# First attention chunk of each image: six additions into the totals moved behind the first slot, two inner sums ahead of it, the last filling's steps split

## The chip, the core and the metric

The kernel runs on one core of a Trainium2 chip. The metric is the device time of one execution in microseconds. Five engines work side by side, each through its own instructions in order: PE (TensorE, matrix products), DVE (VectorE), ACT (ScalarE), POOL (GpSimd) and SP (SyncE). DMA transfers are issued from the queues of SP, ACT and POOL.

## What is computed

Two layers over x of shape (2, 512, 64, 64) in float32. Layer 0 is a deformable convolution on the group-normalized x, added to x. Layer 1, which this change touches, is an attention over the 4096 pixels of each image:

```python
q = jnp.tanh(px @ Wq.T)
k = jnp.tanh(px @ Wk.T)
v = px @ Wv.T
scores = jnp.einsum('bip,bjp,p->bij', q, k, align_w)
attn = jax.nn.softmax(scores, axis=2)
content = px + attn @ v
content = content @ Wfc.T + bfc
```

It is followed by a batch normalization over both images, a ReLU and the addition of the layer's input.

## The kernel before

Layer 0 fills the first 1160 us of the span. Layer 1 then takes the two images one after the other (loop over `n`). For each image there are two stages.

**The value stage.** Four steps `i`, each over two chunks of 512 pixels, compute keys and queries (`pk`), and in four tiles `t` the values already multiplied by `Wfc` (`values`, products `pvx` and `pvy`, L1740). The values are kept in a form for a fast matrix product with seven products in place of eight at two levels: VectorE combines the pieces of two tiles in a generator `filling`, eight steps per pair of tiles, and stores them in DRAM by SP's queue (L1386, L1387). `fill` is a queue of such generators, and `step(count)` runs that many of their steps. `between(1)` and `between(2)` are called by `values` in the midst and at the end of a tile, and each ends in `step(2)`. The steps of the last pair (group 7) are left over when the stage ends.

**The slots.** A `Chunk` is 1024 of the queries, and there are four chunks for each image. Each has 63 slots: seven forms of the fast product (`p`), by eight groups of keys and the residual (`g`). Slot `s` does seven products on PE into `accx` and `accy` (`products`, L1544). It needs a piece `v` from DRAM (`fetch`, three slots ahead, on ACT's queue for the first six slots of an image and on SP's after), a piece of exponentials `e`, and the inner sums `tt` of that piece (`inner_sums`, L1523 and L1524 on VectorE). `sums(s)` makes the inner sums of slot `s`. It runs `LEAD` = 4 slots ahead, and the tiles rotate through five buffers, which they share with the stored sums `vsum` of `filling`.

The exponentials come from `produce`: PE makes scores `pS` (L1451), ACT their exponentials (L1456). They come two pieces at a time at the slots in `EVENTS`, by rows e0, e2, e3, e1. For the first chunk of an image, e0 and e2 are produced in the value stage (`EARLY`). At the next event or slot, `settle` lets VectorE subtract one half of a piece from the other (`transform`, L1441), and for e0 and e2 adds the piece into a running total of the softmax's denominators (`add_total`). That addition is a DMA that accumulates, or, where `direct` is set, one on VectorE:

```python
if direct:
    nc.vector.tensor_add(parts[0], parts[0], t)
else:
    nc.gpsimd.dma_start(parts[0], t, accum_op=ALU.add)
```

`direct` is set for what is produced in the value stage's last step (`i == 3`). In slot 4 the two running totals are merged (`merge`, L1490) and folded (`total`, L1494, L1495). In slot 5, `spread_total` lets PE sum them over the partitions into `pr` (L1499), ahead of that slot's products. The residual of the chunk is loaded on POOL's queue (`at(-7, ...)`), normalized on ACT (`at(-3, ...)`, four instructions L1335) and scaled by `pr` on VectorE (L1515). The second row's total goes the same way in slots 20 to 23.

All of layer 1 stands under a manual schedule: the order of the instructions on each engine is the order in which the program calls them.

Of the kernel before, what the change touches and what calls it, by code (L numbers as in the profile page):

```python
# [529 lines left out]
LEAD = 4  # L530
# [24 lines left out]
def window_path(  # L555
# [70 lines left out]
    with ExitStack() as l0:  # L626
# [384 lines left out]
        class Chain:  # L1011


            def __init__(self, stage, i):
                self.steps = stage(i) if 0 <= i < NSEQ else iter(())
# [219 lines left out]
    with ExitStack() as l1, tc.manual_schedule():  # L1235
# [78 lines left out]
        with ExitStack() as inner:  # L1314
# [106 lines left out]
            class Chunk:  # L1421

                def __init__(self, n, k):
                    self.n, self.k = n, k
                    self.end = n + 1 == NB and k + 1 == NCH // 2
                    self.order = END if self.end else ORDER
                    self.e, self.tot, self.m, self.q = {}, {}, {}, None

            ROW = {"e0": (0, 0), "e1": (0, 1), "e2": (1, 0), "e3": (1, 1)}
            ORDER = (("e0", 0), ("e2", 1), ("e1", 6), ("e3", 4), ("e3", 2), ("e0", 3), ("e2", 5))  # L1430
# [47 lines left out]
            def settle(c, key, g, direct=False):  # L1478

                for k in (g, g + 1):  # L1480
                    e = c.e[key, k]
                    transform(e)
                    if key in ("e0", "e2"):
                        add_total(c, 0, e, direct)
                    if key == "e1":
                        second_row(c, k)

            def merge(c, qh):
                t, u = c.tot[qh]
                nc.vector.tensor_add(t, t, u)  # L1490
# [141 lines left out]
            class Attention:  # L1632
# [45 lines left out]
                def slot(self, s):  # L1678
                    k, l = divmod(s, SLOTS)
                    c = self.chunks[k]  # L1680
                    nxt = self.chunks[k + 1] if k + 1 < NCH // 2 else None
                    self.fetch(s + 3)
                    if l % (NG + 1) == 0 and self.ends:
                        next(self.ends[-1], None)
                    if l == 20:
                        merge(c, 1)
                    self.before(l, c)
                    if nxt and l >= 43:
                        if l == 43:
                            nxt.q = load_queries(self.n, k + 1)  # L1690
                        self.before(l - SLOTS, nxt)
                        self.at(l - SLOTS, nxt, s)
                    self.at(l, c, s)
                    if l == 21:
                        total(c, 1)
                        self.sums(s + 3)
                    if l + LEAD not in (8, 24, 26):
                        self.sums(s + LEAD)
                    if l == 4:
                        merge(c, 0)  # L1700
                        total(c, 0)
                    p, g = divmod(l, NG + 1)
                    products(c, p, g, self.v.pop(s), self.t.pop(s))
                    for e in self.ends[:-1] if g == 0 else self.ends:
                        next(e, None)
                    if g == NG:
                        self.ends = self.ends[-1:] + [collect(c, p, first_copy(c), c.acc)]
# [102 lines left out]
            for n in range(NB):  # L1810
                at = Attention(n)
                first = at.chunks[0]

                for i in range(NCH // 2):
                    if 0 < i < 3 or n and i == 0:
                        k = i + 1 if i else 1
                        pixels[k] = load_pixels(n, k, nc.gpsimd)
                    pk = pair_bank("pk")
                    for h in range(2):
                        for kb in range(KB):  # L1820
                            nc.tensor.matmul(  # L1821
                                pk[:, h, :], wkq[:, kb, h : h + 2].rearrange("p h d -> p (h d)"),
                                pixels[i][h][kb // 2][:, kb % 2, :], start=(kb == 0), stop=(kb == KB - 1),
                            )
                    qt = piece("qt", (P, CH))
                    for h in range(2):
                        rk, rq = slice(h * DQ, (h + 1) * DQ), slice((1 - h) * DQ, (2 - h) * DQ)
                        nc.scalar.activation(qt[rq], pk[rq, h, :], AF.Tanh)
                        nc.scalar.activation(keys[rk, i, :], pk[rk, h, :], AF.Tanh)
                    nc.scalar.activation(qt, qt, AF.Identity, scale=al)  # L1830
                    for h in range(2):
                        nc.scalar.dma_start(q_d[n][i][:, h, :], qt[(1 - h) * DQ : (2 - h) * DQ, :])
                    if i == 0:
                        first.q = load_queries(n, 0)
                    if i:
                        psums[i] = sum_pixels(nc.vector, pixels[i])
                    for t in range(4):
                        if t % 2 == 0:
                            raw = []
                        raw.append(piece("vform", (P, 2, 4, P)))  # L1840

                        def between(stage):
                            event = EARLY.get((i, t))
                            if event and stage == 2:
                                for done in at.open:
                                    settle(*done)
                                produce(first, *event)
                                at.open = [(first, *event, i == 3)]
                            step(2)

                        values(t, pixels[i], psums[i], wc, wcs, raw[-1], between)
                        if t in (1, 2) and i + 1 < NCH // 2:
                            for h in range(2):
                                normalize(pixels[i + 1][t - 1][h], 2 * h, *norms[n])
                        if t % 2:
                            g = 2 * i + t // 2
                            fill.append(filling(*raw, v_d[n][g], piece if g + 1 == NG else None))
                        if i == 3 and t == 2:
                            for s in range(3):
                                at.fetch(s)  # L1860
                    pixels.pop(i)
                    psums.pop(i)
                for s in range(LEAD):
                    at.sums(s)
                for s in range(NCH // 2 * SLOTS):
                    if s == 0:
                        at.at(-7, first, s)
                    if s == 2:
                        at.at(-3, first, s)
                    at.slot(s)  # L1870
                    if s < 5:
                        step(2)
                    if n == 0 and s in (92, 94, 96, 98, 101, 103):
                        next(later, None)
                    l = s - (NCH // 2 - 1) * SLOTS
                    if n + 1 < NB:
                        if l == 47:
                            pixels[0] = load_pixels(n + 1, 0, nc.gpsimd)
                        if l == 49:
                            wc = value_output(nc.sync)  # L1880
                        if l == 51:
                            wcs = sum_value_output(wc)
                        if l in (52, 53):
                            for h in range(2):
                                normalize(pixels[0][l - 52][h], 2 * h, *norms[n + 1])
                        if l == 55:
                            psums[0] = sum_pixels(nc.vector, pixels[0])
                    if n + 1 == NB:
                        check(l)
                    if n + 1 == NB and l >= 22:  # L1890
                        if l == 48:
                            for _ in batch_norm(0):
                                pass
                        if l > 49:
                            put_out(True)
                        if l in (54, 57, 60):
                            put_out(True)
                        if l > 51:
                            refill(nc.gpsimd)
                        if l == 22:  # L1900
                            room = key_tile()
                            spare = deque((room[:, 0:2], room[:, 2:4]))
                        live = 3 + sum(last + g >= l for last in (31, 36, 45, 54) for g in range(NG + 1))
                        if waiting and (spare or live + len(taken) + 2 <= 37):
                            fetch(lambda name: spare.popleft() if spare else ring_piece(name), nc.gpsimd)
# [67 lines left out]
```

## Time and profile before

| | |
|---|---|
| median of 3 runs | 3325.03 us (3322.0 to 3329.67) |
| the profiled execution's own time | 3324.42 us |
| its span | 3322.5 us |
| mean granted clock of PE | 0.98 |
| PE busy | 3144.2 us (95% of the span) |
| DVE busy | 2747.2 us (83%) |
| ACT busy | 1342.1 us (40%) |
| POOL busy | 292.2 us (9%) |
| value stage of image 0, first slot after it | 1162 to 1304 us, 1304.24 us |
| value stage of image 1, first slot after it | about 2208 to 2349 us, 2349.28 us |

A row of the time view gives the start in us from the span's start, the duration, the engine, the line of the kernel, the operation, what it writes and reads, the shapes, and in brackets the idle time of the engine ahead of it with what ended it. A row of the waits gives the waiting engine and instruction, what it waited for, the sum in us, the number of waits and the longest. A row of the windows gives the stretch, its length, the busy time and number of instructions of PE, PE's weight loads, DVE, ACT and POOL, the granted clock of PE, the share of the DMA engines in use, and GB/s.

### The profile page before, as it was taken

What the parts mean: (1) busy time and instruction counts of PE and PEld (TensorE: products, weight loads), DVE (VectorE), ACT (ScalarE), POOL (GpSimd) and SP (SyncE); (2) the same over time, 40 slices, a digit from 0 to 9 for tenths busy, and PEclk for the clock granted to TensorE, in tenths of its full rate; (3) what the DMA queues carried; (4) which work ended last, traced back from release to release, by engine and by line L of the source; (5) the groups of instructions that cost most, each with busy time, mean ns of one, the idle gap of its engine ahead of it and who ended that gap; (6) DMA issues with size and microseconds to landing.
All of it is one profiled execution on the core that took longest, in us unless ns stands there. A gap on an engine that the chain in (4) does not pass through costs nothing. (4 is left out here: it accounts for less than half of the span.)

```text
span 3322.5 us, 38350 instructions
## 1 busy us (share of the span) xinstructions
PE 3144.2 (95%) x14171; PEld 2259.2 (68%) x14171; DVE 2747.2 (83%) x3928; ACT 1342.1 (40%) x1848; POOL 292.2 (9%) x420
## 2 busy tenths in 40 slices
PE   5899999999999899999999999999999999999991
PEld 2455555555555676787877877887687787787781
DVE  7999999999998689885976967968897786886994
ACT  2678887888886533203113122123211202203114
POOL 1100000000000000001000011000001101001022
PEclk9999999999999999999999999999999999999996
DMA  7335543443444278658667677557667758658699
GB/s 240 121 118 155 153 122 112 137 151 108 120 137 139 92 287 258 196 171 224 196 175 215 190 219 202 187 191 245 220 201 207 203 179 239 189 161 238 195 349 374
DMA packets 241237, 632.61 MB, mean 190 GB/s; under 512 B 28528, under 2 KB 45552, under 8 KB 240016
## 3 DMA queue, kind: packets, MB, share of 16 engines
q1 hardware_dynamic: 177136, 415.33, 37.7%
q0 software_dynamic: 51936, 179.86, 20.4%
q10 hardware_dynamic: 11968, 34.87, 2.8%
q8 instruction: 114, 1.87, 0.2%
q14 instruction: 83, 0.68, 0.1%
HBM read 410.15 MB, written 124.91 MB: 161 GB/s over the span
## 5 line engine op out<-in xcount | busy, mean ns | idle before, releaser
L1544 PE MATMUL accy<-tt,v 128*128 128x256 f32 x2016 | 601.7, 380 | 0.7 <-DVE ct L1577 0.6
L1456 ACT ACTIVATE e<-pS 128x1024 f32<-128x1024 f32 x256 | 248.3, 1021 | 737.2 <-PE pS L1451 737.2
L1544 PE MATMUL accx<-e,v 128*128 128x256 f32 x1792 | 471.2, 385 | 0.3 <-ACT e L1456 0.3
L1544 PE MATMUL accy<-e,v 128*128 128x256 f32 x1792 | 461.7, 380 | 0.0
L1544 PEld LDWEIGHTS accy<-tt,v 128*128 128x128 f32 x2016 | 383.8, 191 | 54.2 <-DVE ct L1577 1.0
L1544 PEld LDWEIGHTS accx<-e,v 128*128 128x128 f32 x1792 | 333.5, 190 | 120.4 <-issue 77.7
L806 DVE SCALAR_TENSOR_TENSOR conv<-xn,L_conv_dw_w_sb,conv 128x504 f32<-128x504 f32 (+1 forms) x512 | 376.8, 744 | 29.7 <-ACT conv L798 15.8
L1544 PEld LDWEIGHTS accy<-e,v 128*128 128x128 f32 x1792 | 341.7, 191 | 46.8
L1524 DVE TENSOR_TENSOR tt<-tt,e 128x512 f32<-128x512 f32 x448 | 309.9, 692 | 15.3
L1544 PE MATMUL accx<-tt,v 128*128 128x256 f32 x1008 | 301.2, 380 | 13.1 <-DVE tt L1523 13.1
L1523 DVE TENSOR_TENSOR tt<-e 128x256 f32<-128x256 f32 x448 | 187.7, 419 | 144.8 <-PE accy L1544 142.3
L976 PEld LDWEIGHTS pa<-bt,patch 96*128 96x128 f32 x2048 | 247.6, 195 | 58.1 <-issue 38.2
L976 PE MATMUL pa<-bt,patch 96*128 96x128 f32 x2048 | 251.8, 279 | 8.4 <-issue 3.6
L1451 PE MATMUL pS<-q,keys 64*128 64x512 f32 x1024 | 254.7, 615 | 0.3 <-DVE stats L1729 0.3
L962 ACT COPY bt<-pb 96x1024 f32<-96x1024 f32 x120 | 225.9, 2023 | 50.4 <-PE pb L957 50.4
L772 PE MATMUL pq<-in_w,xn 128*128 128x512 f32 x512 | 234.0, 599 | 3.6 <-ACT xn L762 3.5
L996 PE MATMUL py<-dT,L_conv_out_w_sb 128*128 128x512 f32 x512 | 230.0, 593 | 0.0
L1544 PEld LDWEIGHTS accx<-tt,v 128*128 128x128 f32 x1008 | 191.9, 191 | 40.3 <-DVE tt L1523 14.3
L1549 ACT COPY u<-accx 128x256 f32<-128x256 f32 x56 | 20.8, 372 | 484.2 <-PE accx L1544 477.6
L866 PE MATMUL po<-om_w_pg,feat 128*128 128x432 f32 x512 | 206.4, 548 | 0.8 <-ACT feat L849 0.8
L987 ACT COPY dT<-pa 32x256 f32<-32x256 f32 x496 | 179.9, 363 | 62.9 <-PE pa L976 53.6
L996 PEld LDWEIGHTS py<-dT,L_conv_out_w_sb 128*128 128x128 f32 x512 | 95.5, 190 | 114.3 <-issue 107.4
(274 smaller groups left out, 4266.4 us busy)
## 6 DMA issues: line engine op xcount, KB each, us to landing
v<-wv SPq DMA_DIRECT2D x436, 448.0 KB
tot<-e POOLq DMA_DIRECT2D x160, 512.0 KB, 6.8
patch<-xt SPq DMA_DIRECT2D x256, 192.0 KB
v<-ww SPq DMA_DIRECT2D x56, 448.0 KB
wv<-vform SPq DMA_DIRECT2D x48, 512.0 KB
wv<-vsum SPq DMA_DIRECT2D x48, 384.0 KB
xt<-xj SPq DMA_DIRECT2D x128, 128.0 KB
res<-in_x SPq DMA_DIRECT2D x64, 256.0 KB
```

The lines of the kernel that those rows point to most:

```text
L772: nc.tensor.matmul(pq, xn[:, kb, 1 + 2 * t : 3 + 2 * t, :].rearrange("p r c -> p (r c)"), in_w[:, kb, :], start=(kb == 0), stop=(kb == KB ...
L806: nc.vector.scalar_tensor_tensor(dst, src, wt, dst, ALU.mult, ALU.add)
L866: nc.tensor.matmul(po[:, : 3 * GP], f[:, kb, t * P : (t + 1) * P], om_w[:, kb].rearrange("p a k g -> p (a k g)"), start=(kb == 0), stop=(k ...
L962: copy(bt[:SN].rearrange("s g q d -> s d (g q)")[:, d0 : d0 + 4, :], pb[:SN])
L976: nc.tensor.matmul(pa[:, p], xp[:SN, p, cb * P : (cb + 1) * P], bt[:SN, 4 * cb : 4 * cb + 4, PX * s + p, :], start=True, stop=True,)
L987: copy(dst, src)
L996: nc.tensor.matmul(py, out_w[:, kb, cb * P : (cb + 1) * P], dT[:, kb, :], start=(kb == 0), stop=(kb == KB - 1))
L1451: nc.tensor.matmul(p[:, a, :], keys[r, i, (2 * u + h) * P : (2 * u + h + 1) * P], c.q[r, qh, :], start=True, stop=True,)
L1456: nc.scalar.activation(e.rearrange("p a q -> p (a q)"), p.rearrange("p a q -> p (a q)"), AF.Exp)
L1523: nc.vector.tensor_sub(t[:, 0], x[:, 1], x[:, 3])
L1524: nc.vector.tensor_add(t[:, 1:3], t[:, 0].unsqueeze(1).to_broadcast([P, 2, HQ]), x[:, 0:3:2])
L1544: nc.tensor.matmul(out, v[:, blk, :], op, start=(first and g == 0), stop=(final and g == NG))
```

## The change

- `settle` no longer adds a piece of e2 with `direct` at once. It puts it into a list `later` of its chunk. There are six such pieces in the first chunk of each image: two were added in each of the tiles t = 2 and t = 3 of the last step, and two in slot 0. Slots 1, 2 and 3 now add two each, behind the inner sums of those slots. What is left would be added in slot 4, ahead of the merge.
- The inner sums of slots 0 and 1 are made at the end of the last tile (`between(2)` of `i = 3`, `t = 3`), ahead of the settling, the scores and the filling steps there. Those of slots 2 and 3 stay where all four were, after the value stage.
- The last filling's eight steps came two at a time behind slots 0 to 3. Now two come behind each of slots 0 and 1, one behind slot 2, and one behind each of slots 8, 9 and 10.
- The residual of the first row is normalized ahead of slot 3 in place of slot 2.

```diff
@@ class Chunk
                     self.e, self.tot, self.m, self.q = {}, {}, {}, None
+                    self.later = deque()
@@ def settle
                     if key in ("e0", "e2"):
-                        add_total(c, 0, e, direct)
+                        if direct and key == "e2":
+                            c.later.append(e)
+                        else:
+                            add_total(c, 0, e, direct)
@@ def slot
                     if l + LEAD not in (8, 24, 26):
                         self.sums(s + LEAD)
+                    for _ in range(min(len(c.later), 2 if s else 0)):
+                        add_total(c, 0, c.later.popleft(), True)
                     if l == 4:
+                        while c.later:
+                            add_total(c, 0, c.later.popleft(), True)
                         merge(c, 0)
                         total(c, 0)
@@ def between
                         def between(stage):
+                            if (i, t, stage) == (3, 3, 2):
+                                at.sums(0)
+                                at.sums(1)
                             event = EARLY.get((i, t))
@@ the slots' loop
-                for s in range(LEAD):
+                for s in range(2, LEAD):
                     at.sums(s)
                 for s in range(NCH // 2 * SLOTS):
                     if s == 0:
                         at.at(-7, first, s)
-                    if s == 2:
+                    if s == 3:
                         at.at(-3, first, s)
                     at.slot(s)
-                    if s < 5:
-                        step(2)
+                    if s in (0, 1, 2, 8, 9, 10):
+                        step(2 if s < 2 else 1)
```

## The prediction

> **What bounds the kernel now.** I read the page first: PE is busy 95% of the span, and the chain that ended last is mostly PE, so a microsecond in which PE stands still in the attention part is a microsecond of the run. Second view, PE's waits:
>
> ```profile
> PE accx L1544 <- DVE tt L1523: 13.1, 3, 6.6
> PE pr L1499 <- DVE tot L1495: 7.8, 11, 1.1
> ```
>
> The first row is the largest wait that PE has inside the attention: two of its three are 6.23 us (image 0) and 6.58 us (image 1). The second row is small, but its `pr` is the next thing in PE's queue that depends on VectorE. Third view, PE in order of time around image 0's first slots:
>
> ```profile
> 1304.24 1.10 PE L1544 MATMUL accx<-e,v 128*128 128x256 f32 x4 [0.35 <-ACT e L1456]
> 1311.58 1.22 PE L1544 MATMUL accx<-tt,v 128*128 128x256 f32 x2 [6.23 <-DVE tt L1523]
> ...
> 1332.76 0.59 PE L1544 MATMUL accy<-tt,v 128*128 128x256 f32 x2
> 1333.23 1.10 PE L1499 MATMUL pr<-tot,ones_k 128*128 128x512 f32 x2
> ```
>
> Slot 0 starts at 1304.24, waits for its inner sums until 1311.58, and slot 4's last product (1332.76) is followed at once by `pr`. Fourth view, VectorE in the same stretch:
>
> ```profile
> 1303.94 0.68 DVE L1756 TENSOR_TENSOR u<-u,pvy 128x512 f32<-128x512 f32 x1
> ...
> 1305.60 0.42 DVE L1441 TENSOR_TENSOR e<-e 128x256 f32<-128x256 f32 x1
> 1306.05 1.23 DVE L1463 TENSOR_TENSOR tot<-tot,e 128x1024 f32<-128x1024 f32 x1
> ...
> 1311.10 0.42 DVE L1523 TENSOR_TENSOR tt<-e 128x256 f32<-128x256 f32 x1
> ...
> 1328.36 1.22 DVE L1403 TENSOR_TENSOR vform<-vform 128x1024 f32<-128x1024 f32 x1
> ...
> 1332.66 0.42 DVE L1495 TENSOR_TENSOR tot<-tot 128x256 f32<-128x256 f32 x1
> ```
>
> No row between 1303.94 and 1333.08 has an idle time: VectorE works without a break, and the row total (L1495) that `pr` reads ends at 1333.08, 0.15 us ahead of `pr`. So there are two ends here, the first inner sums and the total, both set by the same saturated engine. Image 1 shows it more sharply, since there PE waits for the total:
>
> ```profile
> 2356.97 1.22 PE L1544 MATMUL accx<-tt,v 128*128 128x256 f32 x2 [6.58 <-DVE tt L1523]
> ...
> 2378.64 1.10 PE L1499 MATMUL pr<-tot,ones_k 128*128 128x512 f32 x2 [0.34 <-DVE tot L1495]
> ```
>
> Last view, the granted clock in stretches of 1 us (PEclk is the number after the five engines):
>
> ```profile
> 1307.00:1308.00 1.00, 0.00 (x0) 0.00 (x0) 0.97 (x3) 0.00 (x0) 0.00 (x0) 0.76 1.06 402
> 1312.00:1313.00 1.00, 1.00 (x3) 0.64 (x3) 0.97 (x3) 0.00 (x0) 0.00 (x0) 0.50 1.04 387
> 1317.00:1318.00 1.00, 1.00 (x5) 0.80 (x4) 0.97 (x3) 1.00 (x2) 0.00 (x0) 0.62 0.72 211
> ```
>
> The stall halves the clock: 0.76 puts its fall at 1307.5 and 0.62 its rise at 1317.8. PE works from 1311.58 to 1317.8 at half speed, 6.2 us, and loses half of that, 3.1 us. In image 1 the same reading gives 2356.97 to 2362.2, 5.25 us, a loss of 2.6 us.
>
> **First inner sums behind the values.** They now follow L1758 of the last tile, and the four additions ahead of them are gone, so VectorE reaches that tile's L1756 earlier: not at 1303.94 but when its last pvy product ends (1301.98; it can't be earlier), say 1302.03; in image 1 at 2347.42 instead of 2349.33. L1523 comes 1.66 us later (0.72+0.60+0.34 by the starts), its result at 1304.1. PE starts slot 0 at 1304.24: the stall of 6.23 us and the cold stretch behind it go from here. What is late next is `pr`.
>
> **PE's arrival at pr.** Five slots of 3.12 us (1321.91 to 1325.03) and two pS groups of 1.92 make 19.44 us: PE has finished slot 4 at 1323.7 instead of 1333.2, and in image 1 at 2349.28+19.44 = 2368.7. v0 to v5 come through ACT's queue; by that queue's traffic v0 to v2 have landed at about 1306.5 and v3 at about 1310. Even late ones would only eat into the wait that now follows.
>
> **VectorE's way to the total.** The six additions (L1463) move, but all stay ahead of `pr`, which is still in slot 5. Removed from ahead of it are only the last form's sums: 0.66 (L1381 and L1382 at 1325.97) and 2.32 us (L1403, L1381, L1382 at 1328.36), 2.98 us. I add up the new order from L1756 by distances between starts: 1.66; sums 0 and 1, 2.12; two transforms 0.67; L1403 to L1382, 2.32; sums 2 and 3, 2.13; transforms 0.67; sums 4, 1.06; filling 1.86; sums 5, 1.06; two additions, 1.26+1.14; filling 1.32; sums 6, 1.06; additions 2.40; filling 1.07; transforms 0.67; sums 7, 1.06; additions 2.52; merge and total 1.25+0.73+0.42. That is 28.45 us (the old order was 29.14 with two additions fewer). `pr` can start at 1302.03+28.45+0.15 = 1330.63 instead of 1333.23, and at 2376.02 instead of 2378.64: 2.60 and 2.62 us earlier, 5.22 us in all. So PE's stall isn't removed: it moves to `pr` and is 6.9 and 7.3 us long.
>
> **The clock behind pr.** The old cold stretch was hidden, since VectorE needed until 1333.08 anyway. The new one lies behind `pr`, where nothing hides it. No row shows a stall there; its cost is bounded by the cold stretches after other stalls: 6.2 and 5.25 us here, and 4.7 us after a wait of 3.64 us at 179.79 (clock 0.97 in 184.5 to 185.0). Half of each is 3.1, 2.6 and 2.4. At the low end stands nothing at all: after 1.76 us idle at 1131 the clock stayed 1.00. A stall of 7 us is nearest to the 6.23 and 6.58 ones; I take the mean of the three, 2.7 us for each image, 5.4 in all. The Trainium skill (TensorE: Matmul & The Clock Gate, "What you observe" and "What's actually happening") has windows of 3.4 us that run freely, an idle one halving the clock and a full busy one restoring it; the clock's two low stretches here (1307.5 to 1317.8, and 2355.4 to 2362.2) are three and two such windows long, and its estimate of 3.4 to 6.8 us cold after a restart, 2.56 us lost on average, would make the sum -0.1 us. The same page's advice against idle gaps over some 3 us speaks against this change, which moves the gap and doesn't close it.
>
> **The late sums.** 0.66 us comes behind slot 8, where VectorE waits 1.87 and 2.66 us; 2.3 us behind slots 9 and 10, in a busy stretch to 1391. That stretch's own waits, 0.52 (1384.22) and 1.77 us (1392.44), take it up; in image 1 they are 0.52, 0.46 and 1.23. Cost nothing; with that cover gone the second `pr` (slot 23, PE waits 0.68 already) would be up to 2.3 us late per image. Their four stores move on SP's queue behind later v loads, and the load for slot 14 behind them: issued at about 1361, needed at 1369.8.
>
> **Rest.** The residual's normalization (ACT, 2.93 us) goes behind slot 2's exponentials and is ready near 1316, needed at `pr`; POOL's queue keeps its order. Inner sums 4 now wait for slot 0's products, whose buffer they take, with all of VectorE's way to the total queued behind them: the products are over by 1308, VectorE gets there at 1311.6. Both cost nothing.
>
> **Sum.** -5.22+5.4 = +0.2 us. Against the profiled execution (3324.42, span 3322.5) that is 3324.6; the median of the runs is 0.6 higher, so 3325.2.
>
> **Rivals.** *The clock holds, or its loss is hidden.* Then -5.2 us remains: 3319.8. For it: 1.76 us idle didn't lower the clock. Against: the waits of 3.64, 6.23 and 6.58 us all did. 0.11.
> *The stall really goes.* If the total were not what PE waits for, both stalls (12.8) and both losses (5.7) would go: 3306.5. It needs the total at 1323.7, 7 us less work on VectorE than the count above; only the additions' place, not their number, changes. 0.07.
> *Slower: VectorE held by a buffer.* Inner sums 2 and 3 write into buffers that the last stores of the group before must have left, issued near 1301 and 1302, while the DMA share is 1.0. VectorE reaches them at 1308.8 and 1309.9 (2355.3 in image 1). In the old run that traffic ends at about 1309.5 and 2355.1. Each microsecond by which they land after 1309.9 goes straight onto `pr`; if they end only with the following burst (1313.3), it is 3.4 us for each image, 6.8 in all: 3332. 0.12.
>
> **How the numbers follow.** Forecast 0.70. A difference under about 0.2% (6.7 us) can't be told from none. Its own spread is the clock's (2.4 to 3.1 twice), up to 2 us for late sums or stores, and the runs' own (3322.0 to 3329.67). Of its 0.70, 0.64 is within 0.2%, 0.02 faster, 0.04 slower; the held clock gives 0.07 same and 0.04 faster; the vanished stall 0.07 faster; the held buffer 0.08 slower and 0.04 same. Faster 0.13, same 0.75, slower 0.12. The range takes in the held clock and most of the held buffer: 3319.0 to 3331.5; outside are the vanished stall and the ends of the others.
>
> **What would show it.** Right: no wait of `accx` for `tt` above 1 us; one of about 7 us of `pr` for L1495, in both images, followed by about 5 us at clock 0.50. Wrong: `pr` waiting under 3 us; the clock at 1.00 behind it; L1523 idle behind a DMA; a second `pr` waiting over 1.5 us.

## The result, and the profile after

| | before | after |
|---|---|---|
| median of 20 runs each, in turn on the same chips | 3325.1 us (3322.0 to 3329.92) | 3330.3 us (3324.45 to 3337.21) |
| ratio of after to before | | 1.0017, 95% interval 1.001 to 1.0023 |
| the profiled execution, its span | 3324.42, 3322.5 us | 3324.45, 3322.7 us |

The change costs 0.17%, 3.3 to 7.6 us by the interval. That is clear of zero; the 0.17% lie under the 0.2% that the prediction took as no change, the interval's upper end (0.23%) doesn't. The profiled execution of after is the fastest of its 20 and the one with the highest granted clock (0.982, the others 0.976 to 0.981), so its span can't be held against the median; the stretches inside it can be measured. Lines have moved: L1523 is L1527, L1490 to L1499 are L1494 to L1503, L1544 is L1548, L1740 and L1756 are L1748 and L1764.

PE's waits in the profile after. Columns: us in total, times, longest.

```profile
PE pr L1503 <- DVE tot L1499: 24.3, 10, 8.2
PE accx L1548 <- DVE tt L1527: 0.2, 1, 0.2
```

The wait of `accx` for the first inner sums (13.1 us before) is gone and the wait of `pr` has grown by 16.5 us: the idle time has moved on. PE in order of time, both images:

```profile
1303.63 1.10 PE L1548 MATMUL accx<-e,v 128*128 128x256 f32 x4 [0.29 <-ACT e L1457]
1331.36 2.04 PE L1503 MATMUL pr<-tot,ones_k 128*128 128x512 f32 x2 [8.15 <-DVE tot L1499]
1403.76 1.10 PE L1503 MATMUL pr<-tot,ones_k 128*128 128x512 f32 x2 [2.42 <-DVE tot L1499]
2376.36 2.05 PE L1503 MATMUL pr<-tot,ones_k 128*128 128x512 f32 x2 [8.19 <-DVE tot L1499]
2447.57 1.10 PE L1503 MATMUL pr<-tot,ones_k 128*128 128x512 f32 x2 [1.50 <-DVE tot L1499]
```

Slot 0 runs through; PE is done with slot 4 at 1331.36-8.15 = 1323.21 and stands still for 8 us in each image. The products of `pr` take 2.04 us in place of 1.10 or so: the clock is halved. New is the wait of the second row's `pr`, 2.42 and 1.50 us, where it was 0.68 in both images before. VectorE in image 0:

```profile
1301.46 0.69 DVE L1764 TENSOR_TENSOR u<-u,pvy 128x512 f32<-128x512 f32 x1 [0.51 <-PE pvy L1748]
...
1303.12 0.42 DVE L1527 TENSOR_TENSOR tt<-e 128x256 f32<-128x256 f32 x1
...
1310.59 0.43 DVE L1527 TENSOR_TENSOR tt<-e 128x256 f32<-128x256 f32 x1 [1.09 <-DMA wv<-vsum]
...
1330.79 0.43 DVE L1499 TENSOR_TENSOR tot<-tot 128x256 f32<-128x256 f32 x1
...
1392.97 1.23 DVE L1494 TENSOR_TENSOR tot<-tot 128x1024 f32<-128x1024 f32 x1 [1.92 <-issue]
```

The inner sums of slot 3 stand 1.09 us behind a store that still reads their buffer; image 1 loses 1.1 us in the same place. All else up to the total is without a break. Much later, the merge of the second row's totals (L1494 in slot 20) waits 1.92 us; before, it ran at 1389.44 without a wait. The clock in stretches of 1 us (PEclk after the five engines) falls at 1328.18 and rises at 1335.0:

```profile
1328.00:1329.00 1.00, 0.00 (x0) 0.00 (x0) 0.97 (x2) 0.00 (x0) 0.00 (x0) 0.59 0.69 197
...
1334.00:1335.00 1.00, 1.00 (x4) 0.77 (x3) 0.97 (x2) 0.00 (x0) 0.00 (x0) 0.50 0.00 0
1335.00:1336.00 1.00, 1.00 (x6) 0.90 (x5) 1.00 (x2) 0.00 (x0) 0.00 (x0) 1.00 0.00 0
```

To compare executions that reach this place at different times, everything below is counted from the end of the image's last pvy product (1301.98 and 2347.37 before, 1301.43 and 2346.56 after). Four distances matter: to the first `pr`; to slot 8 (its first product has `xq`), where the clock has recovered; from slot 8 to the second `pr`; and the sum of the last two against before, which is what the whole region has cost. From the first `pr` to slot 8 PE needs 14.12 us at full clock (45.37-31.25 before); what it takes beyond that is the clock's loss.

### The profile page after: what moved, and what is told of

Same layout as the page of the kernel before. It is cut to its first block, busy times and chain, and to the rows that moved or that the text cites. A ratio compares the mean times of both kernels' runs of the same rounds, so it can differ in the third digit from the quotient of the medians.

```text
span 3322.7 us, 38346 instructions
## 1 busy us (share of the span) xinstructions
PE 3137.1 (94%) x14171; PEld 2255.7 (68%) x14171; DVE 2747.1 (83%) x3928; ACT 1342.9 (40%) x1848; POOL 292.3 (9%) x420
## 4 chain that ended last, share of the span: by engine, by line
PE 79%; DVE 9%; ACT 5%; DMA 4%; issue 2%; SPq 1%; POOL 0%; ACTq 0%; POOLq 0%; DVEq 0%
PE accy L1548 22%; PE accx L1548 17%; PE pa L976 7%; PE pS L1452 6%; PE py L996 6%; PE pq L772 6%; PE po L866 4%; PE pvy L1748 3%; PE pvx L1748 2%; PE pb L957 2%; PE pk L1829 2%; ACT bt L962 1%; DVE conv L806 1%; PE p_mean L822 1%; ACT awT L929 1%
## 5 line engine op out<-in xcount | busy, mean ns | idle before, releaser
L1548 PE MATMUL accy<-tt,v 128*128 128x256 f32 x2016 | 599.8, 379 | 0.7 <-DVE ct L1581 0.6
L1548 PE MATMUL accx<-e,v 128*128 128x256 f32 x1792 | 471.5, 386 | 0.4 <-ACT e L1457 0.3
L1548 PE MATMUL accy<-e,v 128*128 128x256 f32 x1792 | 459.9, 379 | 0.0
L1548 PEld LDWEIGHTS accy<-tt,v 128*128 128x128 f32 x2016 | 382.9, 190 | 53.4 <-DVE ct L1581 1.0
L1548 PEld LDWEIGHTS accx<-e,v 128*128 128x128 f32 x1792 | 333.5, 190 | 121.6 <-issue 79.4
L1548 PEld LDWEIGHTS accy<-e,v 128*128 128x128 f32 x1792 | 340.5, 190 | 46.3
L1527 DVE TENSOR_TENSOR tt<-e 128x256 f32<-128x256 f32 x448 | 187.7, 419 | 146.9 <-PE accy L1548 142.5
L1548 PE MATMUL accx<-tt,v 128*128 128x256 f32 x1008 | 299.9, 379 | 0.2 <-DVE tt L1527 0.2
L1548 PEld LDWEIGHTS accx<-tt,v 128*128 128x128 f32 x1008 | 191.6, 190 | 26.8 <-DVE tt L1527 0.7
```

The source lines that it names most:

```text
L1527: nc.vector.tensor_sub(t[:, 0], x[:, 1], x[:, 3])
L1548: nc.tensor.matmul(out, v[:, blk, :], op, start=(first and g == 0), stop=(final and g == NG))
```

## Experiments

Theory: the run is bound here by VectorE's total, so the stall only moves to `pr`; the change then pays for the clock behind `pr`, for the store that VectorE meets, and for late sums that hold back the second `pr`. Rivals: the clock alone decides; the early inner sums are worth nothing by themselves; the additions' place is what hurts. All distances in us, image 0 / image 1; for the edits see below. Each experiment ran 11 or 12 times, the last two kernels 5 times, beside the kernel before on the same chip (its median there was 3324.61, 3326.61 or 3324.08 us).

| kernel | to first pr | clock's loss behind it | to slot 8 | slot 8 to second pr | region, both images | time, ratio to before (95%) |
|---|---|---|---|---|---|---|
| before | 31.25 / 31.27 | 0 | 45.37 / 45.39 | 54.74 / 54.73 | 0 | |
| after | 29.93 / 29.80 | 1.8 / 1.6 | 45.85 / 45.47 | 56.48 / 55.54 | +3.1 | 1.0017 (1.001 to 1.0023) |
| e_warm | 29.69 / 30.23 | 0 / 0 | 43.85 / 44.38 | 56.02 / 55.53 | -0.5 | 1.0002 (0.9993 to 1.0011) |
| e_678 | 29.12 / 29.48 | 2.0 / 2.7 | 45.22 / 46.26 | 54.74 / 54.73 | +0.7 | 1.0007 (0.9999 to 1.0016) |
| e_order | 28.63 / 28.64 | 1.7 / 2.2 | 44.47 / 44.95 | 56.25 / 55.27 | +0.7 | 1.0004 (0.9995 to 1.0012) |
| e_steps_back | 32.67 / 33.16 | 1.8 / 1.9 | 48.62 / 49.18 | 54.73 / 54.73 | +7.0 | 1.0016 (1.0007 to 1.0025) |
| e_adds_back | 28.28 / 28.78 | 1.6 / 1.7 | 43.98 / 44.60 | 55.95 / 55.59 | -0.1 | 1.0003 (0.9994 to 1.0012) |
| e_late_alone | 31.35 / 31.16 | 0 / 0 | 45.40 / 45.21 | 56.02 / 55.76 | +2.2 | 0.9998 (0.9988 to 1.0007) |
| e_pr6 | 28.79 / 29.84 | 1.7 / 3.0 | 39.46 / 41.84 | 55.86 / 55.59 | -7.5 | 0.9976 (0.9968 to 0.9985) |
| e_b_pr6 | 35.15 / 36.54 | 0 / 0 | 44.17 / 45.55 | 54.73 / 54.74 | -1.0 | 0.9999 (0.999 to 1.0008) |
| e_best_warm | 28.54 / 28.64 | 0 / 0 | 37.56 / 37.66 | 54.73 / 55.26 | -15.0 | 0.9943 (0.9929 to 0.9956) |
| e_best | 28.60 / 28.60 | 0 / 0 | 37.59 / 37.59 | 55.19 / 54.74 | -15.1 | 0.9955 (0.9941 to 0.9968) |

(With `pr` ahead of slot 6 the full-clock distance to slot 8 is 8.99 us.) The region's column lies inside the interval of the time for every kernel but after, whose profile had small losses of the clock and stands 0.2 us below it. The ratios are what is compared; the quotient of two medians differs from them by up to 0.0008.

**Does the clock behind pr cost what was said?** e_warm is after with eight products that nobody reads ahead of the first `pr` of each image, into the unused half of its bank, so that PE isn't idle while it waits:

```diff
-                p = pair_bank("pr")[:, 0, :]
+                pair = pair_bank("pr")
+                p = pair[:, 0, :]
+                if c.k == 0 and qh == 0:
+                    for _ in range(8):
+                        nc.tensor.matmul(pair[:, 1, :], ones, keys[:, 0, :], start=True, stop=True)
```

> The changed kernel with eight idle products (ones times keys, into the unused half of pr's bank, read by nobody) ahead of the first pr of each image. Theory (the stall moved to pr, and half of its price is the lowered clock behind it): PE is busy for some 7.4 us of the 8.2 us that it waited, pr starts within 0.5 us of where it did (28 us after slot 0), the clock stays at 1.00 behind it, and the 1.8 and 1.6 us that the changed kernel's profile lost there, 2.6 on average over executions, are gone: median 5 us below the changed kernel's 3330.3, about 3325. Rival (the clock costs nothing, since VectorE sets the second pr anyway): the median stays at 3330, and what PE gains at slot 5 reappears as a longer wait of the second pr.

Measured: median 3323.43 us beside 3324.61 of before; ratio 1.0002 against the 1.0017 of after. By the ratios about 5 us come back (the two intervals just overlap, near 1.001); in the two profiles the region is 3.6 us shorter, and 3.4 of that is the clock's loss. PE in image 0 (the eight products appear as 16 instructions):

```profile
1320.74 7.03 PE L1506 MATMUL pr<-keys,ones_k 128*128 128x512 f32 x16
1329.14 1.13 PE L1507 MATMUL pr<-tot,ones_k 128*128 128x512 f32 x2 [1.37 <-DVE tot L1499]
```

The granted clock stays 1.00 behind the first `pr` of both images, which now takes 1.13 us. VectorE's side is as in after (buffer waits of 1.05 and 1.52 us; the second `pr` waits 1.97 and 1.47 us). In image 0 that wait of 1.97 us was followed by 3.41 us at half clock (1400.09 to 1403.50), which lies behind the region and isn't in the table. The clock's loss is real, and without it the change is a draw, not a gain.

**Are the late sums free?** e_678 puts the three late steps of the last filling behind slots 6, 7 and 8:

```diff
-                    if s in (0, 1, 2, 8, 9, 10):
+                    if s in (0, 1, 2, 6, 7, 8):
```

> The changed kernel with the last three filling steps behind slots 6, 7 and 8 in place of 8, 9 and 10, where VectorE has waits of 1.7, 1.9 and 2.0 us. Theory (the late sums push the second row's DMA additions and with them the second pr): VectorE reaches slot 10 as early as in the kernel before, the second pr waits 0.7 us in both images in place of 2.42 and 1.50, the first pr is where it was, and the median is 2.6 us below 3330.3: 3327.7. Rival (those waits come from how the DMA additions happened to land in one execution): the second pr still waits 1.5 to 2.5 us, and the median stays at 3330.

Measured: 3326.34 us, ratio 1.0007. The second `pr` in both images:

```profile
1401.68 1.10 PE L1503 MATMUL pr<-tot,ones_k 128*128 128x512 f32 x2 [0.68 <-DVE tot L1499]
...
2445.46 1.10 PE L1503 MATMUL pr<-tot,ones_k 128*128 128x512 f32 x2 [0.68 <-DVE tot L1499]
```

Both are back at 0.68 us, and slot 8 to second `pr` is that of before to 0.01 us. So the place of the late sums, not the early ones or the additions, delays the second `pr`. (In e_best and e_best_warm, which have the same place, it is 0.5 us late in one image each, where the merge waits 1.93 and 1.89 us for the last DMA addition.) The clock took 0.2 and 1.1 us more of this execution than of after, which is why the region gains 2.4 us and no more. How the delay comes about is seen on POOL, whose DMA additions into the second row's total each wait for VectorE. The last of the six, before:

```profile
1381.51 0.86 POOL L1465 DMA_DIRECT2D tot<-e  x1 [2.00 <-DVE tt L1523]
```

and after:

```profile
1383.63 0.86 POOL L1466 DMA_DIRECT2D tot<-e  x1 [2.00 <-DVE tt L1527]
```

All six start 2.1 us later: three of them wait for a subtraction (L1442) on VectorE, and two steps of sums (1.13 and 1.06 us at 1357.33 and 1359.53) now stand ahead of the first of these. From issue to landing the last one takes, before and after (KB, then the time in us):

```profile
tot<-e POOLq DMA_DIRECT2D x1, 512.0 KB, 7.4
```

```profile
tot<-e POOLq DMA_DIRECT2D x1, 512.0 KB, 9.3
```

So it lands at 1392.9, and the merge starts at 1392.97. The profile gives "issue" as its releaser here and the DMA itself in other runs (e_best: 1.93 and 1.07 us behind `DMA tot<-e`). In image 1 the landing takes 8.4 us before and 8.3 after, and the second `pr` is late by less; why the landing in image 0 takes longer stays open.

**Is it the store that holds VectorE?** e_order puts a step of the filling between the inner sums 2 and 3, in place of the one behind slot 0, so that VectorE does other work while the store leaves:

```diff
-                for s in range(2, LEAD):
-                    at.sums(s)
+                at.sums(2)
+                step(2)
+                at.sums(3)
...
-                    if s in (0, 1, 2, 8, 9, 10):
-                        step(2 if s < 2 else 1)
+                    if s in (1, 2, 8, 9, 10):
+                        step(2 if s == 1 else 1)
```

> The changed kernel with the filling's first two steps between inner sums 2 and 3 in place of behind slot 0. Theory (VectorE stands 1.1 us per image for the buffer of inner sums 3, behind the last store): no wait of L1527 for a store, the first pr 1.1 us earlier in each image against the last tile's products, and the median up to 2.2 us lower, 3328. Rival (the second pr is what sets the pace): the first pr earlier, the second where it was, median 3330.

Measured: 3323.33 us, ratio 1.0004. VectorE no longer waits for `wv<-vsum`, and PE's wait is one microsecond shorter in each image:

```profile
1329.06 2.04 PE L1503 MATMUL pr<-tot,ones_k 128*128 128x512 f32 x2 [7.18 <-DVE tot L1499]
...
2372.58 2.05 PE L1503 MATMUL pr<-tot,ones_k 128*128 128x512 f32 x2 [7.18 <-DVE tot L1499]
```

The first `pr` comes 28.63 and 28.64 us behind the last pvy product. The prediction's count was 0.05+28.45+0.15 = 28.65. So the count was right for a VectorE that never waits, and of what it missed in after (1.28 and 1.15 us) the waits for the store are 1.09 and 1.06 us.

**What is each part worth?** Three kernels take the change apart; one with the early inner sums alone, or with the later normalization of the residual alone, was not run. e_steps_back is after with all eight filling steps back behind slots 0 to 3:

```diff
-                    if s in (0, 1, 2, 8, 9, 10):
-                        step(2 if s < 2 else 1)
+                    if s < 5:
+                        step(2)
```

> The changed kernel with the last filling's eight steps where they were before, two behind each of slots 0 to 3. Theory (VectorE's work ahead of the total sets the first pr, the late sums the second): the first pr 3 us later in each image than in the changed kernel (about 33 us behind the last tile's products, PE waiting 11 us), the second pr back at a wait of 0.7 us. Of the 6 us lost some 2.5 come back at the second pr: 3333 to 3334. Rival (the late steps are a loss as a whole): 3328 or less.

Measured: 3332.47 us beside 3326.61, ratio 1.0016. By the times this can't be told from after (1.0017); what follows rests on the traces.

```profile
1337.84 2.04 PE L1503 MATMUL pr<-tot,ones_k 128*128 128x512 f32 x2 [11.16 <-DVE tot L1499]
...
2385.59 2.05 PE L1503 MATMUL pr<-tot,ones_k 128*128 128x512 f32 x2 [11.71 <-DVE tot L1499]
```

PE waits 3 us longer for the total, and the second `pr` is on time again. The late sums have two effects, against each other: in after the total is 2.74 and 3.36 us earlier (2.98 in the prediction), and the time from slot 8 to the second `pr` is 1.75 and 0.81 us longer.

e_adds_back is after with the additions of e2 made at once, as before the change:

```diff
-                        if direct and key == "e2":
-                            c.later.append(e)
-                        else:
-                            add_total(c, 0, e, direct)
+                        add_total(c, 0, e, direct)
```

> The changed kernel with the six additions where they were before, behind their transforms; early inner sums and late steps stay. Theory (the place of the additions ahead of the total decides nothing, since all six stay ahead of it): slot 0 waits about 1 us for its inner sums, pr's wait is that much shorter, and pr itself starts within 0.7 us of the changed kernel's or a little earlier, because VectorE no longer stands idle for the last tile's products; median 3328 to 3330. Rival (moving the additions is what matters): pr 2 us or more later, 3333 or more.

Measured: 3328.32 us, ratio 1.0003. PE waits at two places, each for less:

```profile
1307.61 0.70 PE L1545 MATMUL accx<-tt,v 128*128 128x256 f32 x2 [0.80 <-DVE tt L1524]
1331.81 2.04 PE L1500 MATMUL pr<-tot,ones_k 128*128 128x512 f32 x2 [5.10 <-DVE tot L1496]
...
2351.15 0.70 PE L1545 MATMUL accx<-tt,v 128*128 128x256 f32 x2 [1.61 <-DVE tt L1524]
2375.34 1.35 PE L1500 MATMUL pr<-tot,ones_k 128*128 128x512 f32 x2 [3.41 <-DVE tot L1496]
```

The first `pr` comes 1.65 and 1.02 us earlier than in after, although VectorE starts on the last tile's sums 1.96 us behind the pvy product (in after 0.03). From those sums to `pr` it needs 26.3 us, in after 29.9: two additions (2.4 us) are made ahead of the tile, and it doesn't wait for the store. With the additions moved, VectorE comes to the tile so early that it waits 0.51 us for PE there, and then to the store's buffer before the store has left. In image 1 the wait of 1.61 us at slot 0 halved the clock from 2352.16 to 2355.57:

```profile
2352.00:2353.00 1.00, 1.00 (x3) 0.82 (x4) 0.97 (x3) 0.00 (x0) 0.00 (x0) 0.58 1.07 407
```

What that cost was covered by the wait at `pr`, which is 1.7 us shorter than in image 0. The region is 3.2 us better than that of after; the ratios' intervals (1.0003 and 1.0017) overlap by a little, so the trace shows this and the times agree.

e_late_alone is the kernel before with the late steps alone:

```diff
-                    if s < 5:
-                        step(2)
+                    if s in (0, 1, 2, 8, 9, 10):
+                        step(2 if s < 2 else 1)
```

> The kernel before with one thing of the change: the last three filling steps behind slots 8, 9 and 10. Theory (the late steps by themselves cost at the second pr and bring nothing at the first, which PE reaches no earlier): the first pr within 0.4 us of where it was, the second waits 1.2 to 2.4 us in place of 0.7, and the median is 1.5 to 2.5 us above before's 3324.9. Rival (the second pr's wait has another cause): 0.7 us as before, no difference.

Measured: 3326.45 us beside 3326.61, ratio 0.9998. The time can't tell 2 us from none (its interval reaches to +2.3), the trace can:

```profile
1333.93 1.02 PE L1499 MATMUL pr<-tot,ones_k 128*128 128x512 f32 x2
...
1404.00 1.10 PE L1499 MATMUL pr<-tot,ones_k 128*128 128x512 f32 x2 [1.97 <-DVE tot L1495]
```

The total is earlier and nobody profits, since PE reaches the first `pr` no sooner (31.35 us); the second is 1.3 and 1.0 us late, as with the whole change. Late sums pay only where PE waits for the total, which without the early inner sums it did for no more than 0.34 us (image 1 of before).

**Can the freed time be used?** If PE waits at `pr` for VectorE, the slot behind `pr` can go ahead of it. e_pr6 is after with the first row's `pr` of the first chunk ahead of slot 6 in place of slot 5:

```diff
-                    if l in (5, 23):
-                        spread_total(c, int(l > 5))
+                    if l in (5 if c.k else 6, 23):
+                        spread_total(c, int(l > 6))
```

> The changed kernel with pr of the first chunk's first row ahead of slot 6 in place of slot 5. Theory (the total, not the inner sums, ends the wait, and PE has a slot and a group of scores to do meanwhile): PE's wait at pr falls from 8.2 to about 3 us in each image, no low clock or a short one, slot 8 about 6 us earlier than in the kernel before; the late sums still hold the second pr, so of 12 us some 8 to 10 are left: 3315 to 3318. Rival (VectorE is the bound all the way to the second pr): slot 8 is earlier, but the second pr waits 5 us or more longer, and the median is no lower than 3325.

Measured: 3315.91 us, ratio 0.9976. `pr` starts 1.1 us sooner behind the pvy product than in after in image 0 and as late in image 1, but PE waits 2.40 and 3.35 us for it in place of 8:

```profile
1329.98 1.28 PE L1503 MATMUL pr<-tot,ones_k 128*128 128x512 f32 x2 [2.40 <-DVE tot L1499]
...
2369.15 2.04 PE L1503 MATMUL pr<-tot,ones_k 128*128 128x512 f32 x2 [3.35 <-DVE tot L1499]
```

The clock still fell, in image 0 at 1330.76 and in image 1 at 2368.42; image 0:

```profile
1330.00:1331.00 1.00, 1.00 (x2) 0.43 (x3) 0.96 (x4) 0.00 (x0) 0.00 (x0) 0.88 0.89 355
```

e_b_pr6 makes the same edit in the kernel before.

> The kernel before, with one edit: the pr of the first row's total of each image's first chunk goes ahead of slot 6 instead of slot 5. Theory (the later place only pays because the early inner sums bring PE to slot 5 some 7 us ahead of VectorE): in the kernel before PE reaches pr at 1333.2 with the total ready at 1333.1, so the place changes nothing there: the wait of accx for tt at slot 0 stays at 6.2 and 6.6 us, pr comes one slot later without a wait, slot 8 starts as late as before; 3324 to 3327 us, ratio 0.9995 to 1.0005. Rival (the later place pays by itself, whatever stands ahead of it, as VectorE or the softmax behind pr gains slack): 3317 to 3321 us, as with the early inner sums.

Measured: 3322.34 us beside 3324.08, ratio 0.9999. The waits at slot 0 are those of before (6.6 us), `pr` comes a slot later without a wait for the total, and slot 8 begins 1.2 us sooner in image 0, where the clock rose 3.3 us behind slot 0's stall (6.2 before), and 0.2 us later in image 1. The time shows no difference (the interval is 3 us to either side). So the later place by itself is worth nothing that can be told: it is what turns the early inner sums into a gain.

**A version that beats both.** e_best_warm joins what helped: e_pr6's edit, e_order's, late steps at 6, 7 and 8, and two idle products ahead of `pr`, made as in e_warm. Of its edits only that of the late steps is shown:

```diff
-                    if s in (0, 1, 2, 8, 9, 10):
-                        step(2 if s < 2 else 1)
+                    if s in (1, 2, 6, 7, 8):
+                        step(2 if s == 1 else 1)
```

> The changed kernel with four edits together: pr of the first chunk's first row ahead of slot 6, two idle products (ones times keys, into the unused half of pr's bank) ahead of it, the filling's first two steps between inner sums 2 and 3, its last three steps behind slots 6, 7 and 8. Theory (the four terms add up): pr ahead of slot 6 alone gave 3315.9; the clock stays at 1.00 (1.7 and 3.0 us lost there), the buffer's wait goes (up to 1.1 us per image), and the second pr waits 0.7 us (0.9 to 1.1 us less per image): 3309 to 3312. Rival (VectorE is the bound up to the second pr by then): the second pr waits 2 us or more, and the median is 3314 to 3316.

Measured: 3309.93 us beside 3326.61, ratio 0.9943. e_best is the same without the idle products.

> The version after with pr ahead of slot 6 for the first chunk, the last form's steps behind slots 1, 1, 6, 7 and 8 and a step between the inner sums 2 and 3, without the idle products that kept PE's clock up ahead of pr. It tells what the idle products were worth in the version that measured 3309.9 us. Theory (they keep the clock at 1.00 where a wait of 2.5 us or more would halve it): the first pr waits 1 to 3.5 us, the clock falls in one or both images and costs 1.5 to 3 us for each; 3312 to 3316 us. Rival (a wait of 2 us is too short to matter, the idle products only cost their 2 us): the clock stays 1.00 behind pr in both images, 3308 to 3311 us.

Measured: 3309.62 us beside 3324.08, ratio 0.9955; the rival was right. `pr` and the clock in image 0:

```profile
1335.26 1.10 PE L1503 MATMUL pr<-tot,ones_k 128*128 128x512 f32 x2 [2.22 <-DVE tot L1499]
```

```profile
1335.00:1336.00 1.00, 0.74 (x2) 0.49 (x3) 1.00 (x4) 0.00 (x0) 0.00 (x0) 1.00 1.01 312
1336.00:1337.00 1.00, 1.00 (x5) 0.72 (x4) 0.97 (x3) 0.00 (x0) 0.00 (x0) 1.00 0.98 391
```

A wait of 2.22 us left the clock at 1.00 in both images of this execution, so the idle products had nothing to save there; the two intervals overlap. Either version keeps what the change was able to give: PE passes slot 0 without a wait, and in e_best waits 2.22 us for the total, a time that the idle products fill in e_best_warm.

## Why the prediction was right, and where it was not

The forecast case came: a difference (0.17%) below the 0.2% that the prediction took as none, the stall at slot 0 gone, and another of 8 us at `pr` in both images, with the low clock behind it. That the idle time would move and not go, the mechanism of the forecast, was right. The time, 3330.3 us, lies in the range, though near its upper end and 5.1 us above the number given: two terms failed in the same direction, a third made up for part of it, and the time is still inside because the range had been drawn to take in most of the held buffer. Of the four signs of being wrong two are there: L1523 (now L1527) idle behind a DMA, and in image 0 a second `pr` that waits over 1.5 us. Point by point:

- **PE's arrival at pr** was given as 1323.7 for a pvy product that ends at 1301.98, 21.7 us behind it. It came at 1323.21 for 1301.43: 21.8. Right.
- **VectorE's way to the total**: the count holds to 0.02 us where nothing holds VectorE (e_order). In after it was 1.28 and 1.15 us short, so `pr` gained 1.32+1.47 = 2.8 us in place of 5.2. The step that failed is that `pr` would follow VectorE's work alone. What happened is the rival "VectorE held by a buffer" at a third of its price: the store was over 1.09 and 1.06 us after VectorE came to the buffer, not 3.4.
- **The clock behind pr** was taken as 2.7 us an image, bounded by 2.4 and 3.1. Its cause is shown by e_warm. Its size over twelve restarts in the six kernels that paid it was 1.55 to 3.0 us, on average 2.0: a term mis-sized by 0.7 an image. The profile of after had losses below that average (1.8 and 1.6): of its low stretches of 6.82 us PE worked through only 3.64 and 3.12 us, and the rest fell into the stall itself, where the prediction looked for about 5 us of low clock behind `pr`. The 3.4 to 6.8 us cold and the 2.56 us lost that it calls the Trainium skill's estimate are worked out from the window on that page (TensorE: Matmul & The Clock Gate, "What's actually happening"), which doesn't give them itself; twice the losses here is 3.1 to 6.0 us.
- **The late sums** were to cost nothing, and up to 2.3 us an image without their cover, VectorE's own waits. They cost 1.74 and 0.81 us. As far as VectorE's own work goes, the cover of image 0 would have done: VectorE was ready for the merge 1.7 us later behind slot 8 than before, and 1.77 us of waiting stood behind it. It then waited 1.92 us for the last DMA addition. In image 1 the 0.46 us that the prediction counted as cover is the merge's own wait, which ends with such a landing. The step missed that POOL's chain of DMA additions starts behind the same subtractions, so that a delay of VectorE at 1360 comes back as a wait for a transfer at 1391.
- **The sum** with these sizes is -2.8+2x2.0+2.55 = +3.7 us, against +0.2 predicted and +3.3 to +7.6 measured. In the profiled execution the region costs +3.1 us; that its span is only 0.2 us longer must come from elsewhere, such as waits of 0.93 and 1.09 us at the first `pr` of two later chunks that are in before's profile and not in after's.
- **The rivals**: the clock did not hold, and the total did not come at 1323.7. Against the latter the prediction held that only the additions' place changes; e_adds_back shows that the place is worth 1.0 to 1.65 us at `pr`, for the worse.

## What to carry to other kernels

When two waits of one engine are set by the same saturated engine, taking away the first moves it to the second; find out what PE could do ahead of the second, and move that, or the gain stays locked in (here 0.24% came from one slot placed ahead of `pr`, and nothing without it or without the early sums). Work moved to "a stretch with slack" must be followed along every queue that starts behind it: two sums on VectorE delayed six DMA additions, and a merge 30 us later. To judge changes of a few us, count from an event inside the kernel that the change doesn't touch, not from the span.

## What the runs showed of the hardware

The clock moves on a grid. Its low stretches were 6.82 us in after (1328.18 to 1335.0, and 2372.66 to 2379.48), 3.41 behind the first `pr` in both images of e_adds_back and in image 0 of e_pr6, and 10.24 in e_steps_back: one, two or three times 3.41 us. The Trainium skill (TensorE: Matmul & The Clock Gate, "What's actually happening") has a free-running window of 3413 ns, which agrees. It lets the clock fall after an idle window; here windows that were not wholly idle did it too. PE worked 0.72 us of the 3.41 ahead of the fall at 2376.06 in e_adds_back, about 1.0 us ahead of the one in image 0 of e_pr6, and 1.68 us ahead of the one at 2352.16 in e_adds_back, behind a wait of 1.61 us. The clock did not fall behind a window with 1.96 us of work (e_adds_back, image 0, before 1328.2), nor behind one with 1.43 us (e_best, 1333.28 to 1336.69, which holds its wait of 2.22 us). So neither the length of a wait nor the work in its window alone tells, by these traces, whether the clock falls: a wait of 1.61 us halved it in one kernel, and one of 2.22 us did not in another. What a gap costs behind it lay between nothing and 3 us. That the executions of one kernel spread by this is not shown, but it fits their clocks: the five fastest of the 20 runs of after have a mean granted clock of 0.980 to 0.982, the five slowest 0.976 to 0.980. Single profiles a few us apart say little.
